# Graph attention on one core: the finishing stages of a node pair are spread over the tile slots of two steps

## The chip, the core and the metric

The kernel runs on one core of a Trainium2 chip. The metric is the device time of one execution in microseconds (us). "The time" of a kernel is the median of many executions.

## The reference

The computation is one graph-attention layer with 12500 nodes, 256 features, 8 heads of 32 and 200000 edges, sorted by their target node. Cut to what matters:

```python
h   = relu(layernorm(x))
q, k, v = h @ Wq + bq, h @ Wk + bk, h @ Wv + bv          # (n, 8, 32) each
logits  = einsum('ehd,ehd->eh', q[dst], k[src]) / sqrt(32)
w       = exp(logits - segment_max(logits, dst)[dst])
agg     = segment_sum(w * v[src], dst) / segment_sum(w, dst)
o   = agg + (h @ Wskip + bskip)
y   = h + gelu(o)
out = x + layernorm(y) * gamma + beta
```

The last three lines are what this text calls finishing a node.

## The kernel before

A first stage (`project`) computes `h`, `k|v` and `q` for all nodes and writes them to tables in device memory. A planner sorts out which edges are read when. Then `walk_streams` walks the edges. They are cut into 8 streams; a step `c` (66 of them, `NST`) takes three tiles `j` = 0, 1, 2, and a tile is 128 edges of each of the 8 streams.

For every tile, `gather(c, j)` issues eight indirect DMAs on POOL (line 1027), one per stream; each fetches 128 rows of 2 KB of the table `kv_tab` into one of six `kv` tiles. Then come, per tile:

- `times` (DVE, L1074, two halves): the product of `k` with the queries of the targets, which TensorE has spread into PSUM (`spread`, L1065); half 0 needs the first four gathers of the tile, half 1 all eight. `total` (DVE, L1081) sums it per head. `turn` (PE, L1091) transposes the result.
- once per step, `maxima` (DVE, L1102, L1103, L1105), `exponent` (ACT, L1109), `turn_back`, `weights`, `carried`: the running segment maximum and the weights.
- `weigh(c, j)` (DVE, L1140): `v` times the weights, for 128 x 2048 elements; both inputs lie in SBUF. It is the last reader of the `kv` tile, which a gather of two steps later fills again (`gather_next`). `add_up` (PE, L1164) sums the rows by target; `add_up_results` (ACT L1176, L1182; SP L1186) stores them in `table`.

The order on each engine is the order of the program text (`keep` chains every instruction to the one before on its engine); POOL and SP also issue in program order. On DVE, the three `weigh` of a step divide the order into three slots:

- slot A, from `weigh(c-1, 2)` to `weigh(c, 0)`: `maxima(c)`, then `times(c+1, 0)` and `total`;
- slot B, from `weigh(c, 0)` to `weigh(c, 1)`: `times(c+1, 1)` and `total`;
- slot C, from `weigh(c, 1)` to the next step's `weigh(c, 2)`: `times(c+1, 2)` and `total`.

Finished nodes are handled in pairs of 128-node blocks (class `Pair`), at most one new pair per step, 32 pairs in 39 steps (`FIN_RATE`). A pair is fetched at the end of one step (`fetch`, six DMAs on SP, L836), worked on in the next step (there it is called `pair`) and ended in the step after that (there it is called `before`). Its stages are:

- `turn`, `skip`, `add` (PE L849, L862, L866, L871; copy ACT L852), `divisors`, `divide` (DVE L841, L843, L855), `gelu` (ACT L875);
- `stats` (DVE L878, L882, L884), `root` (ACT L888, a square root), `factors` (DVE L892, L893), `normal` (ACT L898), `shifted` (PE L905, L908), `scale` (DVE L912, L914), `store` (SP L919, two DMAs).

`table_of(f)` (ACT, L986) runs a one-element activation so that the activation table of `f` is loaded at that place. `windows` (SP, L1022) loads the queries of two steps later in eight DMAs, `penalties` (L1008) and `prefetch` (L1002) load small tables. `hot_e` and `hot_n` (PE L1042, L1053; ACT L1044, L1055) make one-hot matrices. PSUM tiles `ps_hot` rotate over two buffers. Four last pairs are finished after the walk by `Last`.

Of the kernel before, what the change touches and what calls it, by code (L numbers as in the profile page):

```python
# [33 lines left out]
AF = mybir.ActivationFunctionType  # L34
# [13 lines left out]
K = 3  # L48
# [16 lines left out]
QT = 6  # L65
# [693 lines left out]
def walk_streams(tc, N, HID, NST, KL, many, ident, idx, d0_row, slot_row, near, near_n, e_tab, pen_tab, h_tab,  # L759
# [48 lines left out]
    class Pair:  # L808
# [25 lines left out]
        def rows_of(self, t, tab, first, used):  # L834

            self.keep(nc.sync.dma_start(t.bitcast(U8), at_byte(tab, first, P, used)))  # L836
# [8 lines left out]
        def turn(self):  # L845
            ps = self.ps_h()
            for b in range(2):
                for c in range(KC):
                    self.keep(nc.tensor.transpose(ps[:, b, c, :], self.h[:, b, c * P:(c + 1) * P],  # L849
                                                  ident))  # L850
            self.hT = self.pool.tile([P, 2, KC, P], F32, name="hT", bufs=1)
            self.keep(nc.scalar.copy(self.hT, ps))  # L852
# [99 lines left out]
    with ExitStack() as es:  # L952
# [31 lines left out]
        def table_of(function):  # L984

            keep(nc.scalar.activation(dummy[:, 1:2], dummy[:, 0:1], function))  # L986

        def tiles_of(c):
            return KL if c == NST - 1 else K
# [42 lines left out]
        def gather_next(c, j):  # L1032

            if c + 2 < NST and j < tiles_of(c + 2):
                gather(c + 2, j)

        def hot_e(c, i):

            if i == 0:
                step[c]["to_e"] = hot.tile([P, QT, CH], F32R, name="to_e")  # L1040
            ps = hot_ps.tile([P, S * WN], F32, name="ps_hot")
            keep(nc.tensor.matmul(ps[:, :CH], near[:, i * P:(i + 1) * P], step[c]["et"],  # L1042
                                  start=True, stop=True))
            keep(nc.scalar.activation(step[c]["to_e"][:, i, :], ps[:, :CH], AF.Relu, scale=-1.0,  # L1044
                                      bias=ones))
# [12 lines left out]
        def spread(c, j, half):  # L1058

            g = step[c]  # L1060
            ps = qe_ps.tile([P, 2, 2, HID], F32, name="ps_qe")
            for a in range(2):
                for b in range(2):
                    i, at, w = rows_of(4 * half + 2 * a + b)
                    keep(nc.tensor.matmul(ps[:, b, a, :],  # L1065
                                          g["to_e"][at:at + w, i, j * P:(j + 1) * P],
                                          g["qw"][at:at + w, i, :], start=True, stop=True))
            g["qe", half] = ps

        def times(c, j, half):  # L1070

            g = step[c]
            k = g["kv"][j][:, 4 * half:4 * half + 4, :HID].rearrange("p (a b) d -> p a b d", a=2)
            keep(nc.vector.tensor_tensor(k, g["qe", half].rearrange("p b a d -> p a b d"), k,  # L1074
                                         op=OP.mult))

        def total(c, j):
            g = step[c]
            if j == 0:
                g["L"] = work.tile([P, K, SH], F32, name="L")  # L1080
            keep(nc.vector.tensor_reduce(g["L"][:, j, :].rearrange("p (s h) -> p s h", s=S),  # L1081
                                         g["kv"][j][:, :, :HID].rearrange(
                                             "p s (h d) -> p s h d", h=HEADS),
                                         AX.X, OP.add))
# [22 lines left out]
        def exponent(c):  # L1107
            W = step[c]["W"]
            keep(nc.scalar.activation(W, W, AF.Exp))  # L1109
# [26 lines left out]
        def weigh(c, j):  # L1136
            g = step[c]
            t = g["vw"][j]
            wj = g["w"][:, j, :].rearrange("p (s h) -> p s h", s=S)
            keep(nc.vector.tensor_tensor(  # L1140
                t[:, :, HEADS:].rearrange("p s (h d) -> p s h d", h=HEADS),
                wj[:, :, :, None].to_broadcast([P, S, HEADS, D]),
                g["kv"][j][:, :, HID:].rearrange("p s (h d) -> p s h d", h=HEADS), op=OP.mult))
            if j == 0:
                keep(nc.vector.tensor_tensor(t[:, :, :HEADS], wj, wden[c % 2], op=OP.mult))
# [99 lines left out]
        pair = before = None  # L1245
        for c in range(NST - 1):

            pair_next = None
            if c in due:
                pair_next = Pair(fin, due[c][0],  # L1250
                                 lambda: hot_ps.tile([P, 2, KC, P], F32, name="ps_hot"),
                                 lambda: ag_ps.tile([P, 2 * HID], F32, name="ps_a").rearrange(
                                     "p (b d) -> p b d", b=2),
                                 keep)
            if c + 2 < NST:
                windows(c + 2)
            for half in range(2):
                times(c, K - 1, half)
                spread(c + 1, 0, half)
            total(c, K - 1)  # L1260
            turn(c, K - 1)
            if c:
                weigh(c - 1, K - 1)
                gather_next(c - 1, K - 1)
            maxima(c)
            if before:
                before.factors()
            if c:
                add_up(c - 1, 0, range(K - 1, K))
                add_up_products(c - 1, 1)  # L1270
            exponent(c)
            turn_back(c)
            if c:
                add_up_results(c - 1, 1)
            weights(c)
            if c:
                add_up(c - 1, 2)
            carried(c)
            for half in range(2):
                times(c + 1, 0, half)  # L1280
                spread(c + 1, 1, half)
            total(c + 1, 0)
            weigh(c, 0)
            gather_next(c, 0)
            for j in range(K):
                hot_n(c, j)
            turn(c + 1, 0)
            if before:
                before.normal()
                before.shifted()  # L1290
            if pair:
                pair.turn()
                pair.divisors()
                pair.divide()
                pair.skip()
            if before:
                before.scale()
                before.store(0)
                before.store(1)
            if pair_next:  # L1300
                pair_next.fetch()
            if c == NST - 2:
                for i in range(4):
                    last(i)
            if c + 2 < NST:
                for i in range(QT // 2):
                    hot_e(c + 2, i)
            if pair:
                pair.add()
                table_of(AF.Gelu)  # L1310
                pair.gelu()
            for half in range(2):
                times(c + 1, 1, half)
                if tiles_of(c + 1) == K:
                    spread(c + 1, K - 1, half)
            total(c + 1, 1)
            turn(c + 1, 1)
            weigh(c, 1)
            gather_next(c, 1)
            if c + 2 < NST:  # L1320
                for i in range(QT // 2, QT):
                    hot_e(c + 2, i)
            add_up(c, 0, range(K - 1))
            if c + 2 < NST:
                penalties(c + 2)
            if c + 3 < NST:
                prefetch(c + 3)
            if c == NST - 2:
                weigh(c, K - 1)
                add_up(c, 0, range(K - 1, K))  # L1330
                add_up(c, 1)
                if pair_next:
                    pair_next.turn()
                    pair_next.skip()
            if pair:
                table_of(AF.Sqrt)
                pair.stats()
                pair.root()
                table_of(AF.Exp)
            if c == NST - 2:  # L1340
                add_up(c, 2)
            before, pair = pair, pair_next
            if c > 1:
                step[c - 2] = None

        c = NST - 1
# [7 lines left out]
            turn(c, K - 1)  # L1354
        maxima(c)
        exponent(c)
        if pair:
            table_of(AF.Gelu)
            pair.divisors()
            pair.divide()  # L1360
        if before:
            before.factors()
        turn_back(c)
        weights(c)
        carried(c)
        weigh(c, 0)
        if pair:
            pair.add()
            pair.gelu()
        if before:  # L1370
# [405 lines left out]
```

## Time and profile before

| | |
|---|---|
| median of 17 runs | 2725.69 us (2721.49 to 2739.56) |
| profiled execution | 2723.23 us, of which the span from first to last instruction is 2721.3 us |
| first and last gather of `kv` in it | start at 355.8 us, last start at 2639.8 us |
| busy: PE / DVE / ACT / POOL | 61% / 73% / 40% / 71% of the span |
| DMA | 649.33 MB, mean 239 GB/s |

Up to 355.8 us the projection and the planner run; then the steps follow each other, some 35 us each; after the last gather comes a tail of some 80 us in which the last pairs are finished. All durations below are of the one profiled execution. Its own time is 2.5 us below the median. "E" in the prediction is the end of the `weigh` that opens slot A.

### The profile page before, as it was taken

How to read it: one execution, taken by the hardware profiler on the slowest of the kernel's cores; microseconds unless marked ns; L12 is line 12 of the kernel's file. 1: busy time of each engine (PE TensorE's matmuls, PEld its weight loads, DVE VectorE, ACT ScalarE, POOL GpSimd, SP SyncE). 2: the span in 40 equal slices, each digit the busy share in tenths (PEclk: the TensorE clock that was granted, in tenths of full speed). 3: DMA queues.
4: the chain of work that ended last, by engine and by line, in shares of the span. 5: the costliest groups of instructions: out<-in, count | busy, mean ns of one | idle time of the engine just before them, and what ended most of it. 6: DMA issues, size and time to landing. Idle time of an engine off the chain costs nothing. (4 is left out here: it accounts for less than half of the span.)

```text
span 2721.3 us, 29239 instructions
## 1 busy us (share of the span) xinstructions
PE 1652.1 (61%) x7824; PEld 857.0 (31%) x7824; DVE 1992.2 (73%) x2330; ACT 1099.1 (40%) x2552; POOL 1942.6 (71%) x1745
## 2 busy tenths in 40 slices
PE   6899944444456656656565555555566566566565
PEld 3455522222223323323233222233233233233233
DVE  7776846666667777877777777777778777778784
ACT  3334322222234434434444434344345344344344
POOL 4432467777777777777777777777777777777760
PEclk9999966555567767767667667667667677677678
DMA  7766677777778878887788788788888888888872
GB/s 238 268 250 242 256 249 221 219 219 216 222 244 256 242 244 241 248 247 233 240 246 254 241 250 254 242 245 253 245 251 242 249 253 241 252 241 256 245 219 70
DMA packets 306127, 649.33 MB, mean 239 GB/s; under 512 B 52836, under 2 KB 192238, under 8 KB 300954
## 3 DMA queue, kind: packets, MB, share of 16 engines
q0 software_dynamic: 128768, 423.23, 51.5%
q1 hardware_dynamic: 176434, 223.46, 25.1%
q8 instruction: 65, 1.06, 0.2%
q14 instruction: 112, 0.92, 0.1%
q10 hardware_dynamic: 748, 0.66, 0.1%
HBM read 538.91 MB, written 108.23 MB: 238 GB/s over the span
## 5 line engine op out<-in xcount | busy, mean ns | idle before, releaser
L1027 POOL DMA_INDIRECT kv<-kv_tab,idx x1576 | 1804.9, 1145 | 482.3 <-issue 439.5
L1074 DVE TENSOR_TENSOR kv<-ps_qe,kv 128x1024 f32<-128x1024 f32 x394 | 478.6, 1221 | 569.6 <-DMA kv<-kv_tab,idx 566.8
L1065 PE MATMUL ps_qe<-qw,to_e 64*128 64x256 f32 (+1 forms) x1576 | 320.0, 397 | 580.5 <-DVE kv L1074 559.4
L1065 PEld LDWEIGHTS ps_qe<-qw,to_e 64*128 64x128 f32 (+1 forms) x1576 | 225.7, 250 | 746.9 <-DVE kv L1074 635.3
L1140 DVE TENSOR_TENSOR vw<-w,kv 128x2048 f32<-128x2048 f32 x197 | 450.0, 2285 | 8.6 <-ACT w L1125 5.6
L1081 DVE TENSOR_REDUCE L<-kv 128x64 f32<-128x2048 f32 x197 | 450.3, 2286 | 6.9 <-DVE kv L1074 0.2
L1044 ACT ACTIVATE to_e<-ps_hot,ones 128x384 fp32r<-128x384 f32 x396 | 212.5, 579 | 470.2 <-PE ps_hot L1042 463.6
L1164 PE MATMUL ps_a<-vw,to_n 128*32 128x264 f32 (+1 forms) x2344 | 315.3, 568 | 117.0 <-DVE vw L1140 115.6
L1176 ACT COPY sums_w<-ps_a 128x264 f32<-128x264 f32 x130 | 49.3, 379 | 788.1 <-PE ps_a L1164 778.0
L268 POOL TENSOR_TENSOR qp<-qp 128x256 fp32r<-128x256 f32 x98 | 89.3, 911 | 170.0 <-ACT qp L267 169.7
L256 PE MATMUL ps_kv<-w_kv,hT 128*128 128x512 f32 x392 | 197.9, 628 | 17.7 <-ACT hT L141 16.7
L1164 PEld LDWEIGHTS ps_a<-vw,to_n 128*32 128x32 f32 (+1 forms) x2344 | 106.3, 151 | 276.2 <-DVE vw L1140 155.6
L1164 PE MATMUL ps_hot<-vw,to_n 128*64 128x264 f32 x808 | 188.6, 635 | 2.3 <-DVE o L914 2.3
L1042 PE MATMUL ps_hot<-et,near 48*128 48x384 bf16 x396 | 139.2, 405 | 69.5 <-ACT to_e L1044 64.9
L986 ACT ACT_TABLE_LOAD x138 | 177.1, 1283 | 2.4
L1091 PE MATMUL ps_x<-ident,L 128*64 128x128 f32 x197 | 72.5, 368 | 160.3 <-DVE L L1081 160.0
L1182 ACT COPY kv<-ps_a 1x264 f32<-1x264 f32 x388 | 143.2, 369 | 6.4
L1164 PEld LDWEIGHTS ps_hot<-vw,to_n 128*64 128x64 f32 x808 | 82.6, 219 | 111.4 <-issue 108.2
L262 PE MATMUL ps_q<-w_q,hT 128*128 128x256 f32 x392 | 104.4, 390 | 17.3 <-DVE qp L266 17.3
L1091 PEld LDWEIGHTS ps_x<-ident,L 128*64 128x64 f32 x197 | 23.8, 121 | 276.0 <-DVE L L1081 190.3
L1055 ACT ACTIVATE to_n<-ps_hot,ones 128x384 f32<-128x384 f32 x197 | 103.2, 579 | 9.6 <-PE ps_hot L1053 7.8
L866 PE MATMUL ps_a<-w_s,hT 128*128 128x256 f32 x368 | 95.4, 404 | 16.9 <-ACT hT L852 16.9
(279 smaller groups left out, 1953.1 us busy)
## 6 DMA issues: line engine op xcount, KB each, us to landing
qw<-q_pc SPq DMA_DIRECT2D x264, 128.0 KB
kv<-kv_tab,idx POOLq DMA_INDIRECT x1576
kv_tab<-kvo SPq DMA_DIRECT2D x16, 1280.0 KB
q_pc<-qp SPq DMA_DIRECT2D x16, 1280.0 KB
qw<-q_pc SPq DMA_DIRECT2D x264, 64.0 KB
table<-sums_w SPq DMA_DIRECT2D x264, 61.9 KB
pen<-pen_tab SPq DMA_DIRECT2D x66, 192.5 KB
sums<-table SPq DMA_DIRECT2D x92, 132.0 KB
```

The costliest lines, as they stand in the source:

```text
L256: ins = nc.tensor.matmul(ps_kv, hT[:, c, :], w_kv[:, c, :], start=c == 0, stop=c == KC - 1)
L262: ins = nc.tensor.matmul(ps_q, hT[:, c, :], w_q[:, c, :], start=c == 0, stop=c == KC - 1)
L986: keep(nc.scalar.activation(dummy[:, 1:2], dummy[:, 0:1], function))
L1027: nc.gpsimd.indirect_dma_start(out=t[:, s, :], out_offset=None, in_=kv_tab[:, :], in_offset=bass.IndirectOffsetOnAxis(ap=idx[:, s, j, c:c ...
L1042: keep(nc.tensor.matmul(ps[:, :CH], near[:, i * P:(i + 1) * P], step[c]["et"], start=True, stop=True))
L1044: keep(nc.scalar.activation(step[c]["to_e"][:, i, :], ps[:, :CH], AF.Relu, scale=-1.0, bias=ones))
L1065: keep(nc.tensor.matmul(ps[:, b, a, :], g["to_e"][at:at + w, i, j * P:(j + 1) * P], g["qw"][at:at + w, i, :], start=True, stop=True))
L1074: keep(nc.vector.tensor_tensor(k, g["qe", half].rearrange("p b a d -> p a b d"), k, op=OP.mult))
L1081: keep(nc.vector.tensor_reduce(g["L"][:, j, :].rearrange("p (s h) -> p s h", s=S), g["kv"][j][:, :, :HID].rearrange("p s (h d) -> p s h d" ...
L1140: keep(nc.vector.tensor_tensor(t[:, :, HEADS:].rearrange("p s (h d) -> p s h d", h=HEADS), wj[:, :, :, None].to_broadcast([P, S, HEADS, D] ...
L1164: keep(nc.tensor.matmul(ps[at:at + w, :], g["to_n"][:, j, i * P + at:i * P + at + w], g["vw"][j][:, s, :], start=j == 0, stop=j == tiles_o ...
L1182: keep(nc.scalar.copy(step[c + 1]["kv"][0][0:1, s, HID - HEADS:], ps[at:at + 1, :]))
```

## The change

Only the order of the stages in `walk_streams` changes; no stage is rewritten. `stats` of a pair leaves the end of the step (slot C) and becomes, one step later, the work behind `maxima` in slot A, where `factors` was. `root` follows in slot B behind `hot_n`, and `factors` behind `divide`; `scale`, `store`, and with them the `fetch` of the next pair, move from slot B to the head of slot C, behind `weigh(c, 1)`. `normal` and `shifted` move back accordingly. The line `table_of(AF.Sqrt)` is dropped; `table_of(AF.Exp)` now follows `gelu`, and is also there in a step that only ends a pair. In the last step, which stands outside the loop, `stats`, `root`, `factors` and `table_of(AF.Gelu)` move in the same way.

```diff
             maxima(c)
             if before:
-                before.factors()
+                before.stats()
...
             turn(c + 1, 0)
             if before:
-                before.normal()
-                before.shifted()
+                before.root()
             if pair:
                 pair.turn()
                 pair.divisors()
                 pair.divide()
                 pair.skip()
+            if before:
+                before.factors()
+            if c + 2 < NST:
+                for i in range(QT // 2):
+                    hot_e(c + 2, i)
+            if before:
+                before.normal()
+            if pair:
+                table_of(AF.Gelu)
+                pair.add()
+                pair.gelu()
+            if pair or before:
+                table_of(AF.Exp)
+            for half in range(2):
+                times(c + 1, 1, half)
+                if tiles_of(c + 1) == K:
+                    spread(c + 1, K - 1, half)
+            total(c + 1, 1)
+            turn(c + 1, 1)
+            if before:
+                before.shifted()
+            weigh(c, 1)
+            gather_next(c, 1)
             if before:
                 before.scale()
                 before.store(0)
...
-            if c + 2 < NST:
-                for i in range(QT // 2):
-                    hot_e(c + 2, i)
-            if pair:
-                pair.add()
-                table_of(AF.Gelu)
-                pair.gelu()
-            for half in range(2):
-                times(c + 1, 1, half)
-                if tiles_of(c + 1) == K:
-                    spread(c + 1, K - 1, half)
-            total(c + 1, 1)
-            turn(c + 1, 1)
-            weigh(c, 1)
-            gather_next(c, 1)
...
-            if pair:
-                table_of(AF.Sqrt)
-                pair.stats()
-                pair.root()
-                table_of(AF.Exp)
...
         exponent(c)
+        if before:
+            before.stats()
         if pair:
-            table_of(AF.Gelu)
             pair.divisors()
             pair.divide()
-        if before:
-            before.factors()
         turn_back(c)
         weights(c)
         carried(c)
+        if before:
+            before.root()
         weigh(c, 0)
+        if before:
+            before.factors()
         if pair:
+            table_of(AF.Gelu)
             pair.add()
             pair.gelu()
```

## The prediction

> **What bounds the kernel now.** I read the page first, then POOL, DVE and SP each in order of time.
>
> ```profile
> PE 1652.1 (61%) x7824; PEld 857.0 (31%) x7824; DVE 1992.2 (73%) x2330; ACT 1099.1 (40%) x2552; POOL 1942.6 (71%) x1745
> ...
> L1027 POOL DMA_INDIRECT kv<-kv_tab,idx x1576 | 1804.9, 1145 | 482.3 <-issue 439.5
> L1074 DVE TENSOR_TENSOR kv<-ps_qe,kv 128x1024 f32<-128x1024 f32 x394 | 478.6, 1221 | 569.6 <-DMA kv<-kv_tab,idx 566.8
> ```
>
> No engine is full, and DVE waits 566.8 us for gathers. POOL never waits longer than 0.3 us between two gathers ("issue"): it issues without pause. One stretch of it:
>
> ```profile
> 1513.22 0.95 POOL L1027 DMA_INDIRECT kv<-kv_tab,idx  x1 [0.31 <-issue]
> 1514.47 2.63 POOL L1027 DMA_INDIRECT kv<-kv_tab,idx  x1 [0.30 <-issue]
> 1517.41 0.95 POOL L1027 DMA_INDIRECT kv<-kv_tab,idx  x1 [0.30 <-DVE ps_x L1102]
> 1518.66 0.95 POOL L1027 DMA_INDIRECT kv<-kv_tab,idx  x1 [0.30 <-issue]
> ```
>
> And DVE beside it:
>
> ```profile
> 1510.54 1.22 DVE L1074 TENSOR_TENSOR kv<-ps_qe,kv 128x1024 f32<-128x1024 f32 x1 [4.41 <-DMA kv<-kv_tab,idx]
> 1511.79 2.29 DVE L1081 TENSOR_REDUCE L<-kv 128x64 f32<-128x2048 f32 x1
> 1514.00 2.28 DVE L1140 TENSOR_TENSOR vw<-w,kv 128x2048 f32<-128x2048 f32 x1
> ...
> 1518.65 0.15 DVE L892 RECIPROCAL rstd<-rstd 128x2 f32<-128x2 f32 x1
> 1518.83 0.16 DVE L893 SCALAR_TENSOR_TENSOR nm<-mv,rstd 128x2 f32<-128x2 f32 x1
> 1519.01 2.52 DVE L1074 TENSOR_TENSOR kv<-ps_qe,kv 128x1024 f32<-128x1024 f32 x2
> ...
> 1531.43 1.23 DVE L1074 TENSOR_TENSOR kv<-ps_qe,kv 128x1024 f32<-128x1024 f32 x1 [1.10 <-DMA kv<-kv_tab,idx]
> ```
>
> The reader is to see that the gather begun at 1514.47, inside `weigh` (1514.00 to 1516.28), takes 2.63 us instead of 0.95 and ends 0.82 us after `weigh`. Counted over the trace, 196 of the 197 `weigh` lengthen just one gather: one that starts up to 20 ns after `weigh` is untouched, from 39 ns on it ends 0.83 us after `weigh`. The lengthened ones are nearly all the sixth to eighth of their tile, though only the first waits for a `weigh`, and that first starts 11 us or more after the `weigh` that it needs. So this is a collision of two engines and no wait. 260 gathers begun inside a half of `times` and 292 inside `total` are not lengthened.
>
> The walk is therefore POOL's: 1576 x 1.258 us = 1983, plus 303 us of lengthening (1.54 a piece), is its 2285 us, 355.8 to 2640.7. Finishing work is otherwise free: steps with it and without both take about 35 us.
>
> A collision costs 2.28 + 0.83 - 0.95 - x = 2.16 - x, where x (0.04 to 1.28 us) is how long after the start of `weigh` the next gather starts. If the slot's `times` last waited for data, `weigh` starts 1.26 + 2.20 us after the landing, and gathers start 0.30 + 1.258 n after the tile's eighth gather: x = (4.39 - lag) modulo 1.258, lag being from that gather's end to the landing. The rows obey it within 20 ns. Mean collision and median lag by slot:
>
> - 35 steps with a pair begun and one ended: A 1.65 (lag 2.89 where waited for), B 1.47 (3.17), C 1.51 (4.90)
> - 9 steps with only one ended: A 1.80, B 1.56, C 1.40
> - 11 steps with neither: A 1.51, B 1.78 (2.78), C 1.62
>
> **The change, part by part.** What moves a `weigh`, a lag or the tail counts; all else hides under POOL.
>
> *DVE in slot A.* `factors` (0.36 from start to start) goes, `stats` (1.71, from L878 at 1503.19 to the next `times` at 1504.90) comes: +1.36. Behind it are `times(c+1,0)`, `total`, `weigh(c,0)`, and for the last the gather that refills the tile, which has 11 us to spare. Where no data are awaited, `weigh(c,0)` starts at E + 7.33 now (next gather at 7.42: the dearest phase, 2.07) and would start at E + 8.69, with a gather at 8.68 just escaped and the next at 9.94: 0.91. That needs the landing before E + 5.2, where half 1 of `times` would be ready.
>
> *SP.* The queue is passed in order:
>
> ```profile
> 1517.91 6.51 SPq L1186 DMA_DIRECT2D table<-sums_w  x8
> 1529.23 3.79 SPq L919 DMA_DIRECT2D out_dram<-o  x2
> 1533.07 0.60 SPq L1008 DMA_DIRECT2D pen<-pen_tab  x1
> 1533.78 0.52 SPq L1002 DMA_DIRECT2D et<-e_tab  x1
> 1535.10 4.77 SPq L1022 DMA_DIRECT2D qw<-q_pc  x8
> ```
>
> The stores wait for `scale`, now behind `weigh(c,1)`: from E + 12.5 to E + 19.9 + 2.28 + 1.3 = 23.5. Everything queued behind moves along: second store +3.6 (27.1), six fetches (28 to 30.5), `penalties`, `prefetch`, and the eight `windows` at 32.8 to 37.7, which is 1.9 us before to 3 us after the next E (35 us a step). The table stores slip from 1.6 to 3.7 us after E. Nobody waits: `windows` and tables are used about a step later, the fetched rows some 15 us later. But the traffic changes its tile. The 11 quiet steps show what B is without stores: 1.78. C takes what B has (stores half a microsecond before its last gather ends, as now in B): lag near 3.2. A gets what C has (`windows` in its last gathers): lag 4 to 4.9, landing at about E + 2.1 + 4.4 = 6.5, past 5.2. So A waits for data again.
>
> Sum of the walk: B 35 x 0.31 + 9 x 0.22 = +12.8; A like C 35 x (1.51 - 1.65) + 9 x (1.51 - 1.80) = -7.5; C like B 35 x (1.47 - 1.51) + 9 x (1.56 - 1.40) = 0. Together +5.3 us. A lag misjudged by 0.3 moves one slot by 13 us; three such give about +-23.
>
> *DVE in B and C.* B loses `scale` (1.41) and gains `factors`; C gets `scale` for `stats`. Both slots wait for data (means 2.08 and 4.52 us), so nothing. `factors` waits for `root`, which on ACT stands behind L1093 and a table load (1.28 + 0.28): ready about 0.4 us before DVE gets there; 1 us late would still be in the wait.
>
> *ACT.* The dropped line saves a dummy, not a load: `root` now brings its own. In the built order loads at L986 go from 138 to 102 and at L888 from 3 to 48: nine more, +9 x 1.28 - 36 x 0.20 = +4.3 us on an engine 40% busy that waits 778 us at L1176. Zero, at worst those 4.3.
>
> *A new collision?* L878 has two SBUF inputs like `weigh`, and moves to E + 2.37, where a gather starts: the recip now there (L892) starts 7 to 29 ns (median 17) before it, and untouched ends at 20. I take zero; 7 of 44 lie past 20, so up to 4 us. Were all caught, 0.68 + 0.83 - 0.95 = 0.55 each, 24 us. In the Trainium skill, "SBUF — State Buffer", "Who interferes with whom", a DVE instruction with two SBUF inputs contends with a GpSimd instruction that reads SBUF: this speaks against the change, and by it any L878 begun first would be caught, +24 us. The same section infers that `tensor_tensor` does not stall descriptor generation; the 196 lengthened gathers here say otherwise.
>
> *Tail.* Before, `fetch` of the last looped pair is issued at 2645.1 to 2647.9, PE turns its rows at 2655.6, ACT copies them at 2656.82 (on the chain that ended last). Now the stores come behind `weigh(64,1)` (2649.4) and `scale` (2650.8); second store +3.2, fetch 2654.9 to 2657.7, its last row block some 2 us later (from the 3 us a store takes to be acknowledged, an estimate): PE at 2659.5, copy +3.3. Off the chain goes the Gelu load before `weights` (1.48; the transposes it hid take 0.6 of it back, plus a few tenths): -0.5. `stats` fills DVE's 5.59 us idle. Net +2.8, between 0 (rows land as early as PE is free) and +4.5.
>
> Total: 2723.2 + 5.3 + 2.8 = 2731.3 for a profiled execution; the median of runs lies 2.5 higher, 2734.
>
> **The rivals.**
>
> *A no longer waits for data* (the queue slips less, or lag stays near 2.9): every `weigh(c,0)` sits at the cheap phase. A 35 x (0.91 - 1.65) + 9 x (0.91 - 1.80) = -33.9; with B and tail 2723.2 - 33.9 + 12.8 + 2.8 = 2705 profiled, 2707 median. For it: E + 2.1 + 2.9 = 5.0 is just early enough. Against: `windows` run beside those gathers, and there C shows 4.90. It decides below a lag of 3.1.
>
> *Phases even out.* All 44 x 3 collisions at the uniform mean 1.50: 35 x (4.50 - 4.63) + 9 x (4.50 - 4.76) = -6.9, tail +2.8: 2719 profiled, 2722 median. For it: C's lags spread over 3.8 to 5.7, more than a full period. Against: quiet B is narrow.
>
> *L878 collides*: main case + 24 = 2758, if its start moves 10 ns earlier against the gathers.
>
> *The label is wrong about loads*: it is, as counted; price 0 to 4.3, within the rest.
>
> **How the numbers follow.** Main case 0.45, A free of data 0.23, phases even 0.20, L878 0.07, 0.05 for the rest. A median can be told from no change at about 0.2%, 5.5 us. Faster: A free and a quarter of the even case, 0.28. Same: half of even, part of main, 0.20. Slower 0.52. Range: from the first rival to the main case plus its 23 us: 2706 to 2757. Faster and slower both hold much; the main case's own range is 2711 to 2757.
>
> **What would show it.** Right: gathers still back to back at 1.258 us, 197 long ones; B's mean near 1.78 and its lag near 2.8; `qw` issued around E; A waiting for data; hT of the last looped pair 3 us later against the last gather. Wrong: A's `weigh` at E + 8.69 without wait (faster); a gather of 1.5 us beside L878 (slower); POOL idle over 0.3 us, which would mean that DVE has become late for the refill.

## The result and the profile after

| | before | after |
|---|---|---|
| median | 2727.26 us (40 runs) | 2764.67 us (7 runs, 2757.35 to 2765.99) |
| ratio, 95% interval | | 1.0130 (1.0117 to 1.0144) |
| span of the profiled execution | 2721.3 us | 2761.2 us |
| last gather to the end | 80.6 us | 84.8 us |

The changed kernel is slower by 1.3%, outside the predicted range of 2706 to 2757 us. The sign was the predicted one; of the times in the prediction, that of the rival "L878 collides" (2758) is the nearest.

On the page after, POOL's gathers are 34.8 us longer, and DVE waits 17 us more for them; the columns are busy time, mean ns, idle time and what ended it.

```profile
PE 1795.7 (65%) x7824; PEld 928.7 (34%) x7824; DVE 1991.4 (72%) x2330; ACT 1105.4 (40%) x2525; POOL 1977.3 (72%) x1745
...
L1027 POOL DMA_INDIRECT kv<-kv_tab,idx x1576 | 1839.7, 1167 | 482.4 <-issue 441.7
L1074 DVE TENSOR_TENSOR kv<-ps_qe,kv 128x1024 f32<-128x1024 f32 x394 | 480.3, 1221 | 598.0 <-DMA kv<-kv_tab,idx 583.7
```

The idle time before gathers is unchanged (482.4 against 482.3): POOL still issues without pause, and each gather that lasts longer moves the end. Which ones do is seen in POOL's order of time after (start, length, then the instruction, and in brackets the idle time before it):

```profile
1517.19 0.95 POOL L1027 DMA_INDIRECT kv<-kv_tab,idx  x1 [0.30 <-issue]
1518.44 2.78 POOL L1027 DMA_INDIRECT kv<-kv_tab,idx  x1 [0.30 <-issue]
1521.52 0.95 POOL L1027 DMA_INDIRECT kv<-kv_tab,idx  x1 [0.30 <-issue]
1522.78 1.49 POOL L1027 DMA_INDIRECT kv<-kv_tab,idx  x1 [0.30 <-issue]
1524.57 0.95 POOL L1027 DMA_INDIRECT kv<-kv_tab,idx  x1 [0.30 <-DVE mv L884]
```

and DVE beside it:

```profile
1518.11 2.28 DVE L1140 TENSOR_TENSOR vw<-w,kv 128x2048 f32<-128x2048 f32 x1
...
1522.29 0.55 DVE L1105 TENSOR_TENSOR W<-ps_x,M 64x384 f32<-64x384 f32 x1
1522.77 0.67 DVE L878 TENSOR_TENSOR sums<-sums,h 128x512 f32<-128x512 f32 x1
1523.47 0.75 DVE L882 BATCH_NORM_STATS2 st<-sums 128x6 f32<-128x256 f32 x2
...
1529.60 1.23 DVE L1074 TENSOR_TENSOR kv<-ps_qe,kv 128x1024 f32<-128x1024 f32 x1 [3.93 <-DMA kv<-kv_tab,idx]
```

The gather of 2.78 us is the known collision with `weigh` (1518.11 to 1520.39). The one of 1.49 us is new: it begins some 10 ns after L878 and ends 0.83 us after it. That L878 meets it in every step that ends a pair is no chance: `weigh` lets its gather go 0.83 us after E, so the next two begin at E + 1.13 and E + 2.39, and L878, two scans and a subtraction of fixed length behind `weigh`, begins at E + 2.37. All 44 L878 inside the walk lengthen one, from 0.954 to 1.49 us: 44 x 0.536 = 23.6 us.

SP's queue after, as predicted in order (stores at a median of E + 25.1, predicted 23.5; fetches 29.4 to 31.8; `windows` around the next E, which is 1520.39 here; the table stores 5.7 us after it, predicted 3.7):

```profile
1514.73 0.35 SPq L836 DMA_DIRECT2D sums<-table  x1
...
1519.52 5.89 SPq L1022 DMA_DIRECT2D qw<-q_pc  x8
1526.15 4.82 SPq L1186 DMA_DIRECT2D table<-sums_w  x8
1545.71 2.52 SPq L919 DMA_DIRECT2D out_dram<-o  x2
```

The 39.8 us between the two spans, in full:

| term | predicted | measured in the profiles |
|---|---|---|
| gathers held by L878 | 0 | +23.6 |
| gathers held by `weigh` (302.6 to 315.1) | +5.3 | +12.5 |
| behind the last gather (80.6 to 84.8) | +2.8 | +4.2 |
| ahead of the first gather, and small remainders | 0 | -0.5 |

### The profile page after: what moved, and what is told of

Read it like the earlier page. It is cut to its first block, busy times and chain, and to the rows that moved or that the text cites. A ratio compares the mean times of both kernels' runs of the same rounds, so it can differ in the third digit from the quotient of the medians.

```text
span 2761.2 us, 29082 instructions
## 1 busy us (share of the span) xinstructions
PE 1795.7 (65%) x7824; PEld 928.7 (34%) x7824; DVE 1991.4 (72%) x2330; ACT 1105.4 (40%) x2525; POOL 1977.3 (72%) x1745
## 5 line engine op out<-in xcount | busy, mean ns | idle before, releaser
L1027 POOL DMA_INDIRECT kv<-kv_tab,idx x1576 | 1839.7, 1167 | 482.4 <-issue 441.7
L1042 PE MATMUL ps_hot<-et,near 48*128 48x384 bf16 x396 | 152.1, 422 | 128.5 <-ACT to_e L1044 123.1
L866 PE MATMUL ps_a<-w_s,hT 128*128 128x256 f32 x368 | 166.4, 630 | 44.9 <-ACT hT L852 43.7
L866 PEld LDWEIGHTS ps_a<-w_s,hT 128*128 128x128 f32 x368 | 111.5, 317 | 88.9 <-ACT hT L852 65.0
```

What stands on the lines that cost most here:

```text
L866: self.keep(nc.tensor.matmul(self.ps[:, b, :], self.hT[:, b, c, :], w_s[:, c, :], start=False, stop=False, skip_group_check=True))
L1027: nc.gpsimd.indirect_dma_start(out=t[:, s, :], out_offset=None, in_=kv_tab[:, :], in_offset=bass.IndirectOffsetOnAxis(ap=idx[:, s, j, c:c ...
```

## The experiments

In these, "held" means a gather lengthened by a DVE instruction, and the walk is the time from the first gather to the last.

### Can the gather be freed by a few ns?

One copy of one element is put ahead of `stats` in the changed kernel (e1_nudge_after), so that L878 starts some 60 ns later, behind the gather.

```
+                nudged[1] = copy(nudged[0])      # DVE, one element
                 before.stats()
```

> The changed kernel with one more DVE instruction: in every step that ends a pair, a copy of one element (some 60 ns, estimated from the shortest DVE rows) stands in front of `stats`, so that L878 starts after the gather beside it and not 17 ns before. Collision theory (in the changed kernel each of 44 L878 lengthens a gather by 0.54 us, 23.6 us in all, and POOL is never idle, so this is paid in full): no gather longer than 1 us beside L878, time 23 us below the changed kernel's 2764.7, so about 2741. Queue theory (the loss comes from the stores, fetches and windows that moved behind `weigh(c,1)`; a lengthened gather is made up for while DVE waits for data): the same 2764.7, or 2 to 3 us more for the added instructions.

Measured 2765.8 us, ratio 1.0162 (1.0142 to 1.0181). It did not do what it was made for. DVE and POOL of this kernel:

```profile
1526.78 0.13 DVE L989 COPY nudged<-nudged 1x1 f32<-1x1 f32 x1
1526.84 0.67 DVE L878 TENSOR_TENSOR sums<-sums,h 128x512 f32<-128x512 f32 x1
```

```profile
1525.54 0.95 POOL L1034 DMA_INDIRECT kv<-kv_tab,idx  x1 [0.30 <-issue]
1526.80 1.54 POOL L1034 DMA_INDIRECT kv<-kv_tab,idx  x1 [0.30 <-issue]
```

The gather now begins 31 to 50 ns before L878 and is held all the same, 44 times, 26.1 us. So the run says nothing on the price of the hold, but it shows that the limit which I had read off `weigh` does not hold for L878 in this place.

### The moved transfers alone

The kernel before, with only `shifted`, `scale`, the stores and the fetch moved behind `weigh(c,1)`; `stats`, `root` and `factors` stay (e2_scale_late).

```
             if before:
                 before.normal()
-                before.shifted()
...
+            if before:
+                before.shifted()
             weigh(c, 1)
             gather_next(c, 1)
+            (scale, both stores, fetch, the four `last`: as in the change)
```

> The kernel before with one part of the change alone: `shifted`, `scale`, `store` and the `fetch` behind them move behind `weigh(c,1)`; `stats`, `root`, `factors` and the tables stay. Collision theory: no new long gathers; only the `weigh` collisions change with the lags (between 0 and +13 us) and the tail is about 3 us later: 2730 to 2743, and far less than the changed kernel's +37. Queue theory: nearly the whole loss, about 2760.

Measured 2739.76 us, ratio 1.0065 (1.0046 to 1.0084). L878 holds nothing here; the gathers held by `weigh` cost 310.8 us (+8.2), the part behind the last gather 86.2 (+5.6). By the ratios, the moved transfers make half of the change's 1.3%; by the spans of the two profiles a third (13.8 of 39.8 us).

### Adding work to shift the phase

Two copies of one element are put ahead of `factors` in the kernel before (e3_nudge_before), so that `weigh(c,0)`, where it waits for nothing, starts just behind a gather's start and not just ahead of it.

```
+                nudged[1] = copy(nudged[0])
+                nudged[1] = copy(nudged[0])
                 before.factors()
```

> The kernel before with two one-element DVE copies in front of `factors` (slot A, steps that end a pair). In 13 of its 44 such steps `weigh(c,0)` starts 0.09 to 0.13 us before a gather and takes the dearest collision (2.06 us); 0.12 us or more later it should start behind that gather and cost 0.93. Collision theory: 13 x 1.13 = 15 us less, some 8 steps that escape already lose up to 0.15 us each: about 2727 - 14 = 2713. Queue theory, or any in which DVE work only adds: no gain, 2727 or up to 5 us more.

Measured 2715.47 us, ratio 0.9967 (0.9951 to 0.9983). DVE and POOL of this kernel:

```profile
1511.27 0.31 DVE L989 COPY nudged<-nudged 1x1 f32<-1x1 f32 x2
...
1516.45 2.28 DVE L1147 TENSOR_TENSOR vw<-w,kv 128x2048 f32<-128x2048 f32 x1
```

```profile
1516.32 0.95 POOL L1034 DMA_INDIRECT kv<-kv_tab,idx  x1 [0.30 <-issue]
1517.58 1.98 POOL L1034 DMA_INDIRECT kv<-kv_tab,idx  x1 [0.30 <-issue]
```

The gather of 1516.32 has escaped, and the next is held for only 1.98 - 0.95 = 1.03 us, where before this place cost 2.07. Slot A's mean falls from 1.65 to 1.26 us in the steps with a pair begun and one ended. Slot B gave 11 of the 16 us back. The sum had said 14 us less, and the medians differ by 8. More DVE work made the kernel faster: the phase model is right in kind, but it did not foresee what slot B gave back.

### One input less in SBUF

`weigh(c,0)` of the kernel before reads its weights from the PSUM tile from which ACT copies them to SBUF, so it has one SBUF input (e4_psum_weights).

```
+            wv = (g["xt"][:, :SH].rearrange("p (s h) -> p s h", s=S) if j == 0 else wj)
...
-                wj[:, :, :, None].to_broadcast([P, S, HEADS, D]),
+                wv[:, :, :, None].to_broadcast([P, S, HEADS, D]),
```

> The kernel before, but `weigh(c,0)` reads its weights from the PSUM tile where the transposes left them, not from their SBUF copy; it is the same instruction with one SBUF input instead of two. If two SBUF inputs are what stops the gather, the 66 collisions of slot A (107.9 us in the profile of before) vanish, the small operations that were shielded by them may collide instead (up to some 12 us): about 2727 - 96 = 2631, and the walk is shorter by that. If any long DVE instruction on SBUF stops the gather, or the walk is bound by the transfers and not by POOL's issue: no change, 2727, with as many long gathers, or with POOL idle in place of them.

Measured 2621.59 us, ratio 0.9625 (0.9601 to 0.9648). The page of this kernel, gathers and both forms of `weigh`:

```profile
L1027 POOL DMA_INDIRECT kv<-kv_tab,idx x1576 | 1703.3, 1081 | 482.4 <-issue 431.6
...
L1141 DVE TENSOR_TENSOR vw<-w,kv 128x2048 f32<-128x2048 f32 x131 | 299.1, 2283 | 0.0
...
L1141 DVE TENSOR_TENSOR vw<-ps_x,kv 128x2048 f32<-128x2048 f32 x66 | 150.7, 2284 | 10.7 <-ACT w L1125 5.6
```

`weigh` takes the same 2.28 us from PSUM, but 124 gathers begin inside the `ps_x` form and none is held by it, while 128 are held inside the others. So the hold comes from the second SBUF input. L912, L878 and L855, which have two SBUF inputs too, now hold 30 gathers, 8.3 us in all (expected: up to 12). In the Trainium skill, "SBUF — State Buffer", "Who interferes with whom", a DVE instruction with at most one SBUF input, outside the modes that use two ports, does not contend with GpSimd; these 124 gathers agree.

### L878 out of the gathers' way

The changed kernel with `stats` ahead of `maxima` (e5_stats_first). L878 then runs in the time in which the gather that `weigh` held is still at work, as it did in the kernel before.

```
             if before:
                 before.stats()
             (moved from behind to ahead of)
             maxima(c)
```

> The changed kernel with `stats` in front of `maxima` and not behind it. L878 then starts right behind `weigh`, while the gather that `weigh` held is still finishing, where no gather starts; DVE has the same work in slot A. The copy added in e1 did not free the gather (it was still held, 44 times, 0.59 us each), so e1 told nothing of the price. Collision theory: no gather held by L878, 23.6 us less than the changed kernel: about 2741, near e2. Queue theory (stores, fetches, windows) or ACT theory (table load in front of the copy of hT): no change, about 2765.

Beside it stand three more kernels. The changed kernel with four reductions of two elements ahead of `stats` (e6_reduce_nudge):

> The changed kernel with four two-element reductions on DVE in front of `stats`, some 0.24 us from the 60 ns that one instruction added in e1, so that the gather starts 0.2 us or more before L878 and not 17 ns after. Collision theory: no gather held by L878, about 2741 although DVE has 176 instructions more. Rival: L878 holds any gather that is under way, whatever its start; then it is still held and the time stays at 2765 or above.

The kernel before with all three `weigh` reading PSUM, the weights kept in columns of the PSUM tile which nothing writes until then (e7_psum_all):

> The kernel before with all three `weigh` of a step reading their weights from PSUM (128 columns of the bank that the transposes leave free hold those of tiles 1 and 2); one more small ACT copy per step. If POOL's issue is the bound: the 197 collisions (303 us) go, the small two-input operations, no longer in the shade of a `weigh`, bring some back (46 x 3 at 0.15 to 0.27 us: 20 to 37 us): 2724 - 303 + 30, about 2450. If the transfers bind once POOL is faster (268 GB/s is the highest slice of before, for the some 550 MB of the walk): about 2500.

And e5 with `penalties`, `prefetch` and `windows` issued ahead of the stores and the fetch (e8_windows_first):

> e5 with the queue put right: `penalties`, `prefetch` and `windows` (called one step earlier) are issued on SP in front of the stores, at the place of `weigh(c,1)`, not behind stores and fetches. If slot A waits for data in the changed kernel because `windows` run beside its last gathers (lag 4.6 against 2.9), the lag falls back to about 3, slot A loses most of its waits, and `weigh(c,0)` sits at the cheap phase in most of the 44 steps: about 2741 - 25 = 2716. If the lag comes from stores and fetches, or the phases only average out: as e5, about 2741 give or take 8.

The times of these four decide nothing. They were taken on a chip on which the kernel before took 3037.56 us: 3060.89 (e5, ratio 1.0053), 3054.61 (e6, 1.0057), 3231.3 (e7, 1.0667) and 3043.09 us (e8, 1.0044). Two more chips were of this kind (kernel before 3024.33 and 3009.26 us): e5 1.0105 and 1.0129, e8 1.0044 and 1.0032, e7 1.0638 and 1.0695; and, on the first of these two, the changed kernel with `weigh(c,0)` from PSUM (e9_after_psum), 3129.55 us, 1.0332:

> The changed kernel with weigh(c,0) alone reading its weights from PSUM. The same edit in the kernel before gave 2621.6 us. Theory (the change's loss is holds by L878, dearer phases in slot B and the tail, none of them in weigh(c,0)): L878 still holds 44 gathers, 2621.6 + 23.6 + 12.8 + 4.3 = 2662 us. Rival (the loss is a wait for data in slot A): it is the same 40 us or less only where POOL waits; with POOL's walk free of weigh(c,0), 2622 to 2635 us.

Why the times decide nothing can be read from the page of e7 on the chip of 3009.26 us:

```profile
L1028 POOL DMA_INDIRECT kv<-kv_tab,idx x1576 | 1532.5, 972 | 1236.6 <-issue 448.6
...
L1147 DVE TENSOR_TENSOR vw<-ps_x,kv 128x2048 f32<-128x2048 f32 x197 | 451.4, 2292 | 953.6 <-ACT kv L1189 459.2
```

The holds by `weigh` are gone (972 ns a gather, against 1145), but POOL is idle for 1237 us before gathers and not for 482; the profile puts 302 us of these waits down to `weigh` and 464 us to two lines of ACT. POOL is not the bound there, so the time does not show the price of its holds. What is slower on these chips, and why e7 is even slower there than the kernel before, is open.

The traces of e6 and e9 tell one thing all the same: where POOL waits, gathers begin at all offsets from L878, so that the limit can be read off. In e6, with reductions ahead of L878, all 34 gathers that began 0.08 us or more before L878 and were still at work take 0.95 us, and the 22 that began 0.12 to 0.51 us after its start are held; so the rival "any gather that is under way" is wrong. In e9, L878 stands right behind L1105 as in the changed kernel. There 34 gathers are held, begun from 0.31 us before L878 to 0.49 us after its start; the 22 that began 0.33 us or more before it go free. The two nearest to the limit, the first free and the second held:

```profile
1053.80 0.96 POOL L1027 DMA_INDIRECT kv<-kv_tab,idx  x1 [0.30 <-issue]
1054.13 0.67 DVE L878 TENSOR_TENSOR sums<-sums,h 128x512 f32<-128x512 f32 x1
...
2925.39 1.81 POOL L1027 DMA_INDIRECT kv<-kv_tab,idx  x1 [0.30 <-issue]
2925.70 0.67 DVE L878 TENSOR_TENSOR sums<-sums,h 128x512 f32<-128x512 f32 x1
```

This chip is not the one of the changed kernel, but the gather and L878 take the same 0.95 and 0.67 us on both. If the limit is the same too, the gather in the changed kernel, 10 to 27 ns after L878, lies 0.3 us inside it, and the shift of e1 by some 60 ns could not free it.

On one more chip the kernel before took 2728.96 us, and e5, e8 and e7 were repeated there (e5d, e8d, e7d). For e5:

> The changed kernel with stats ahead of maxima: L878 runs from E + 0.03 to E + 0.71, inside the time in which the gather caught by the weigh still works. Where POOL bounds the kernel (the kernel before near 2725): theory (L878's hold) 2741 us, ratio 1.005; rival (moved transfers) 2760 to 2768, ratio 1.013. Where POOL waits for its tiles (the kernel before near 3000) the time tells nothing on either.

Measured 2737.54 us (12 runs), ratio 1.0030 (1.0016 to 1.0044). The page of this kernel has

```profile
L1027 POOL DMA_INDIRECT kv<-kv_tab,idx x1576 | 1817.9, 1154 | 482.4 <-issue 440.8
```

and its DVE

```profile
1512.48 2.28 DVE L1140 TENSOR_TENSOR vw<-w,kv 128x2048 f32<-128x2048 f32 x1
1514.68 0.68 DVE L878 TENSOR_TENSOR sums<-sums,h 128x512 f32<-128x512 f32 x1
```

beside this gather, the only long one near it:

```profile
1512.88 2.70 POOL L1027 DMA_INDIRECT kv<-kv_tab,idx  x1 [0.31 <-issue]
```

It ends at 1515.58, 0.82 us after `weigh` and with no regard to L878. No L878 holds a gather; those held by `weigh` cost 315.6 us, as in the changed kernel (315.1). Gathers take 21.8 us less in all, the walk is 21.8 us shorter, and the ratio falls by 1.0%, some 27 us, with an uncertainty of some 5. The theory's sum was 23.6. The part behind the last gather (86.1 us against 84.8) hardly moves. Moving one group of five small instructions by 2.4 us takes back most of the change's loss: this is the test of the cause.

### Is slot A's wait due to `windows`?

e8 on the same chip:

> As the last kernel, with penalties, prefetch and the eight windows issued on SP ahead of the stores and the fetch. Where POOL bounds the kernel: theory (the windows beside slot A's last gathers make it wait for data) 2716 us, ratio 0.996; rival (another cause) 2735 to 2745, as the last kernel.

Measured 2731.99 us, ratio 1.0008 (0.9995 to 1.0020): the same as before, and neither theory's number. The wait did go: `weigh(c,0)`'s tile in the 35 steps with two pairs waits 0.55 us in the mean where e5 waits 2.00. So the wait came with the place of `windows` in SP's queue; `penalties` and `prefetch`, which are smaller, moved with them and were not tried alone. But the gain was not there. DVE of this kernel, slot A of one step, with E at 1516.93:

```profile
1516.85 0.69 DVE L878 TENSOR_TENSOR sums<-sums,h 128x512 f32<-128x512 f32 x1
...
1523.27 2.29 DVE L1081 TENSOR_REDUCE L<-kv 128x64 f32<-128x2048 f32 x1
1526.11 2.29 DVE L1140 TENSOR_TENSOR vw<-w,kv 128x2048 f32<-128x2048 f32 x1 [0.56 <-ACT kv L1182]
```

Here `weigh` waits for ACT and starts at E + 9.18, with a gather at E + 9.93; in 17 of the 44 steps that end a pair nothing holds it and it starts at E + 8.54, 0.14 us ahead of the gather at E + 8.68, the dearest phase. The cheap phase that I had counted on was at E + 8.69. Slot A's mean is 1.67 us, no better than e5's 1.62. What e8 gained on e5 (5.5 us) lies behind the last gather (80.8 us against 86.1), which I had not expected and did not take apart.

### The whole of the lengthening

And e7, also the fastest version found:

> The kernel before with all three weigh reading their weights from PSUM. Where POOL bounds the kernel: 2451 us if nothing else comes late, 2520 to 2620 if data or tiles do. In either case gathers beside a weigh take 0.95 to 0.97 us and POOL's busy time falls from 1805 to about 1530 us.

Measured 2447.85 us, ratio 0.8982 (0.8960 to 0.9003); the sum said 2451. The page of this kernel:

```profile
PE 1659.2 (68%) x7824; PEld 871.0 (36%) x7824; DVE 2002.9 (82%) x2330; ACT 1109.4 (45%) x2618; POOL 1654.6 (68%) x1745
...
L1028 POOL DMA_INDIRECT kv<-kv_tab,idx x1576 | 1517.5, 963 | 487.3 <-issue 432.0
...
L1147 DVE TENSOR_TENSOR vw<-ps_x,kv 128x2048 f32<-128x2048 f32 x197 | 451.0, 2290 | 152.5 <-PE ps_x L1092 139.2
```

1517.5 us for 1576 gathers, 287 less than before: all of the 303 is gone but for 16 us of holds by L912, L878 and L855 (the expectation of e7 said 20 to 37). POOL's idle time is up by 5 us only, so POOL is still the bound. The walk is 2002.5 us: 1576 x 1.258 = 1983, the 16, and some 4 of waits.

## Why the prediction was wrong

**What bounds the kernel: right.** The prediction's count of 196 gathers lengthened by a `weigh` is 193 in the trace: the last four `weigh` start behind the last gather. The sum of 303 us stands. POOL issues without pause in every profile on the chips of this speed, and each term above is a term of its walk or of the part behind it.

**The step that failed: "A new collision? I take zero".** I had the place right: L878 at E + 2.37, a gather there, 7 to 29 ns (median 17) after it; after, it is 10 to 27, median 17. I had the price of the worst case right, 24 us. I chose zero because `weigh` lets a gather go that begins up to 20 ns after it, and took this limit over to another instruction behind another neighbour. L878 held all 44. e9 shows how far off this limit is behind L1105: there a gather is held that began 0.31 us before L878, and only those that began 0.33 us or more before it went free. By this, a start 10 ns earlier or later, which the prediction weighed, could not matter. The chance given to this rival, 0.07, rested on that one borrowed number; the shape of L878, two SBUF inputs like `weigh`, spoke for it. The Trainium skill's rule, quoted in the prediction as what speaks against the change, would have given +24 us, and the runs give +23.6 by the trace and some 27 by e5d. That the kernel became slower was forecast, but by terms that make 16.7 of the 39.8 us; the greater part of the loss came from the one put at zero.

**Slot phases, mis-sized: +5.3 became +12.5.** By slot, from the means of the four kinds of step: A -5.9 (predicted -7.5), B +11.4 (predicted +12.8), C +7.3 (predicted 0). B is quiet as predicted (lag 2.73 for 2.8), and A waits as predicted (lag 4.74, within 4 to 4.9). C's lag is 2.97, where I took 3.2: 4.39 - 3.2 = 1.19 is the cheap end of x, 4.39 - 2.97 = 1.42 is past one period and so x = 0.16, the dear end. This is within the bound that I gave for a lag misjudged by 0.3.

**Rival "A no longer waits": its price was wrong too.** After, an unhindered `weigh(c,0)` starts at E + 8.64, with a gather at E + 9.21 and not at 8.68: the hold by L878 has shifted all gathers behind it by 0.53 us. Nor was the gather at 8.68 sure to escape: 8.64, where 8.69 was predicted, lies 0.04 us ahead of it, and in e5d and e8d, where no hold shifts it, `weigh(c,0)` starts at E + 8.54 and catches it. e8d shows the rival's condition met without its gain.

**Behind the last gather: +2.8 became +4.2**, within the bounds of 0 and 4.5. hT of the last looped pair comes 18.6 us after the last gather's end where it came at 16.1 (+2.5, predicted +3); hT is the transposed rows that ACT copies at L852. Where the other 1.7 us arise was not taken apart.

**Table loads: right.** ACT's groups after, of which before had 138 and 1:

```profile
L986 ACT ACT_TABLE_LOAD x102 | 130.9, 1283 | 1.8
L888 ACT ACT_TABLE_LOAD x46 | 59.0, 1283 | 0.8
```

That is 148 loads for 139 (the prediction counted two loads of other lines, there before and after, to L888), nine more and not one less per pair, and the terms above leave no time for them.

## What to carry to other kernels

Where a queue that is issued without pause bounds the kernel, ask of every instruction which can hold that queue when it starts against the queue's beat, and give a fixed offset near such a beat the price of a hit, not of a miss: it is met in every step or in none. A limit measured on one instruction isn't that of another, nor that of the same one behind another neighbour: here the limit of `weigh` was 20 ns after its start, and that of L878 behind L1105 some 0.3 us ahead of its start. And before ordering collisions by hand, look for the operand that makes them: one input in another memory was worth 10% where POOL bounds the kernel, eight times what the whole rescheduling cost.

## What the runs showed that I had not expected

In e7d whoever is first goes on and the other waits. L878 sits there behind a `weigh` that holds nothing, and meets gathers at all offsets: begun up to 31 ns after L878, they take 0.95 us, and L878 itself grows from 682 ns to as much as 755; begun 41 ns or more after, they are held and L878 takes 682. In the changed kernel gathers begun only 10 to 27 ns after L878 are held and L878 takes 673 ns, in e1 even gathers begun 31 to 50 ns before it, and in e9 up to 0.31 us before it. So the edge lies elsewhere behind L1105 or the copy than behind `weigh`; behind the reductions of e6 it lies between 0.08 us before and 0.12 us after. In the Trainium skill, "SBUF — State Buffer", "Who interferes with whom", the order of issue decides who blocks. e7d agrees; in e9 a gather with the earlier recorded start waits, so the start in the profile is not what decides, and what sets the edge is open.

The same program took some 2725 us on some chips and 3009 to 3038 on others (the kernel before). On the former POOL issues without pause; on the latter, in the traces of the other kernels, it waits for its tiles. e7 is 10% faster on the one and 6 to 7% slower on the others. A version should be timed on more than one chip.
